# A perceiver layer on one core: the span attention's minimum, and the steps behind it, written into other stretches of the half batches

## The chip, the cores and the metric

The kernel runs on one core of a Trainium2 chip, in 32-bit floating point. A core has five engines with a queue each: TensorE (PE, with its weight loads shown apart as PEld), VectorE (DVE), ScalarE (ACT), GpSimd (POOL) and SyncE (SP), which here only issues DMAs. PSUM, into which TensorE writes, has eight banks; VectorE and ScalarE read them, GpSimd doesn't. The metric is the device time of one execution in microseconds (us), as the median of several runs.

## The reference

The input x has 32 batches of 64 rows of 256, the context 32 batches of 1601 rows of 256. One layer is computed, in three parts, each added to x:

```python
x = x + cross_attention(layernorm(x), ctx)   # 16 heads of 16, mask, softmax over 1601 keys
x = x + span_attention(layernorm(x))         # below
x = x + ffn(layernorm(x))                    # a shared gated layer and 8 experts, 2 for each row
```

Span attention gives each row and head a mean and a softness, and attends within the batch's 64 rows:

```python
span = h @ W_span.T                      # two numbers for each row and head
mean = sigmoid(span[..., 0]) * 64
soft = softplus(span[..., 1])
scores = -soft[..., None] * (pos - mean[..., None]) ** 2
attn = softmax(scores)                   # over 64 positions
out = (attn @ value) @ W_out.T           # value = h @ W_val.T, by heads
```

## The kernel before

**Half batches.** Cross attention is done for 8 heads at a time: a half batch n is (batch b, c = 0 or 1), 64 in all, in the loop at L763. Within one pass of the loop TensorE computes the scores of half batch n + 1, the keys and values of batch b + 1, and the values' products of half batch n - 1, while the softmax of n is under way:

- `scores` (L529): the 13 blocks of 124 keys in three groups of 4, 5 and 4, one PSUM bank for each of four head pairs (and, for the group of 5, one more bank and the spare half of another). VectorE adds the mask and takes them to the buffer `prob` (L570, and L563 for the fifth block), between them the running maxima over blocks (`maximum`, L587, into `mrun`, the last into `mx`); the first of the maxima is a copy on ScalarE (`first_maxima`, L579).
- `turned_maxima` (L594, pm) transposes `mx` on TensorE as soon as it is there, `maxima_of_rows` (L601) reduces on VectorE, `maxima_along_rows` (L609 on TensorE, copy mb L613 on ScalarE) spreads the result.
- `less_maxima` (L618) subtracts on GpSimd, four times; `exponentials` (L623) follows on ScalarE, four times, the last one in the next pass of the loop.
- `values` (L633) multiplies by the values, in two rounds of 104 small products; `project_keys` and `project_values` (L492) make keys and values of the next batch, and ScalarE copies them out (kT L507, v L524).

**The order is written out by hand** (`manual_schedule`, L729): each of PE, DVE, Activation and Pool executes its instructions in the order in which the program writes them. The pool of PSUM banks for all of this, `ps_x` (L392), has 6 banks; `mm_bank` takes one for each product, and it comes free when its reader has run.

**The stretches.** A pass of the loop has three stretches. In the first, `run(3n)` stands behind the first subtraction of maxima and before the second round of `values`; in the second, `steps(1)` stands behind the key and value projections and the second subtraction, before the exponential of pair 1; in the third, `steps(2)` stands at the end. `run` (L695) executes what is on the agenda for that stretch, in the order in which it was put there, and each generator says how many stretches later its next step is due.

**Tiles.** Two batches make a tile t of 128 rows (16 tiles). When the last half batch of a tile is done (`finish_steps`, L702), `span_steps` (L242) is put on the agenda. It has 23 steps, and the tables STEPS, LAST_BUT_TWO, LAST_BUT_ONE and LAST (L231 to L236) give the stretch of each, counted from the half batch 4t + 4; the last three are those of tiles 13, 14 and 15. The steps by their index in the tables:

| index | step | engine, line |
|---|---|---|
| 0 | output product po, addition to x, statistics | PE L248, DVE L251, L197 |
| 1 to 3 | spread, norm xn_h, transposition tr_h and copy to hT | POOL L205, ACT L214, PE L221, ACT L260 |
| 4, 5 | psp, span and z; exponential of z | PE L264, DVE L270, ACT L278 |
| 6 | sixteen small operations to mean and soft ("held") | DVE L291 to L303 |
| 7 | difference of positions and mean | POOL L308 |
| 8 | square; product with soft | ACT L312, POOL L313 |
| 9 | minimum `least` over 64 positions | DVE L316 |
| 10 to 13 | exponentials with their sums, 4 heads a step | ACT L320 |
| 14, 15 | reciprocal of the sums; product with it | DVE L325, POOL L327 |
| 16 | values pval, copies to vbd | PE L336, ACT L343 |
| 17 | transposition psa of the probabilities, copies to aT | PE L354, ACT L356 |
| 18, 19 | products po2 and po3, addition to x, statistics, x_kept | PE L364, L374, DVE L377, SP L379 |
| 20 to 22 | spread, norm xn_f, transposition tr_f and copies to xfT | POOL L205, ACT L214, PE L221, ACT L387 |

A tile's steps reach over 24 stretches and a new tile begins every 12, so two tiles are under way at a time: stretch 15 of one tile is stretch 3 of the next. The queries of a later tile (`query_steps`, L449) run at stretches 3 to 7 too (norm xn_q, transposition tr_q, copy xnT L458, product pq, four copies L471). `sc`, on which steps 7 to 17 work, has one buffer.

**The end.** In the last half batch (L826 on) there are no more projections; TensorE fills in the shared gated layer (`unit`, L675, reads xfT; `gate`, L678, on ScalarE and VectorE) between the last tiles' steps, at stretches given by the tables `begin` and `gated` (L847). Then follow the experts (L912, L930), 84 us of TensorE.

## Time and profile before

| | |
|---|---|
| median of 3 runs | 1527.41 us (1525.89 to 1528.43) |
| the profiled execution | 1530.65 us, of which the trace spans 1528.8 us |
| mean granted TensorE clock | 0.992 |
| busy share of the span | PE 96%, PEld 70%, DVE 80%, POOL 73%, ACT 62% |
| chain that ended last | PE 77%, DVE 18%, ACT 2%, issue 2% |
| half batches in the steady part | 20.4 to 22.0 us each |
| from the last pm (1360.31) to the experts (1442.39) | 82 us |

A row of a timeline gives the start (us from the first instruction), the time taken, engine, line, operation, output <- inputs with their shapes, and the number of like instructions; in brackets stands how long the engine had idled before, and what ended that. A row of the waits gives the idle time in all, how often, and the longest. A row for a stretch of time gives its length, then the busy time of PE, PEld, DVE, ACT and POOL with the number of instructions, the granted clock of TensorE (1.00 is full speed), the share of the DMA engines and GB/s.

### The profile page before, as it was taken

How to read it: one execution, taken by the hardware profiler on the slowest of the kernel's cores; microseconds unless marked ns; L12 is line 12 of the kernel's file. 1: busy time of each engine (PE TensorE's matmuls, PEld its weight loads, DVE VectorE, ACT ScalarE, POOL GpSimd, SP SyncE). 2: the span in 40 equal slices, each digit the busy share in tenths (PEclk: the TensorE clock that was granted, in tenths of full speed). 3: DMA queues.
4: the chain of work that ended last, by engine and by line, in shares of the span. 5: the costliest groups of instructions: out<-in, count | busy, mean ns of one | idle time of the engine just before them, and what ended most of it. 6: DMA issues, size and time to landing. Idle time of an engine off the chain costs nothing.

```text
span 1528.8 us, 62985 instructions
## 1 busy us (share of the span) xinstructions
PE 1469.1 (96%) x28600; PEld 1069.2 (70%) x28600; DVE 1224.9 (80%) x2332; ACT 947.6 (62%) x1725; POOL 1121.4 (73%) x508
## 2 busy tenths in 40 slices
PE   8999999999999999999999999999999999988999
PEld 5677767677776767776767767676777777654587
DVE  4889898989888898989898888988898888873100
ACT  3565667666767666666757676666766676756311
POOL 1777788888787878888887878777888778852700
PEclk9999999999999999999999999999999999999899
DMA  5111111111111101111111111011111111005100
GB/s 173 44 37 46 46 46 46 50 38 49 49 49 50 45 25 40 53 46 44 44 50 49 50 49 46 23 42 53 37 51 46 49 46 36 3 6 159 59 28 28
DMA packets 52076, 73.82 MB, mean 48 GB/s; under 512 B 3812, under 2 KB 51040, under 8 KB 51680
## 3 DMA queue, kind: packets, MB, share of 16 engines
q1 hardware_dynamic: 50992, 69.00, 14.8%
q8 instruction: 225, 3.69, 1.0%
q10 hardware_dynamic: 816, 0.79, 0.2%
q14 instruction: 43, 0.35, 0.1%
HBM read 65.57 MB, written 4.19 MB: 46 GB/s over the span
## 4 chain that ended last, share of the span: by engine, by line
PE 77%; DVE 18%; ACT 2%; issue 2%; DMA 0%; POOL 0%; ACTq 0%; POOLq 0%; DVEq 0%
PE pk L492 20%; PE pv L492 18%; PE psc L546 11%; PE pvs L633 10%; DVE mrun L587 8%; DVE prob L570 5%; PE py L930 4%; PE pm L594 2%; PE u L662 2%; PE pb L609 2%; PE ph L912 2%; DVE least L316 1%; PE pq L463 1%; PE psa L354 1%; PE po L248 1%
## 5 line engine op out<-in xcount | busy, mean ns | idle before, releaser
L618 POOL TENSOR_TENSOR prob<-prob,mb 124x1664 f32<-124x1664 f32 x252 | 939.5, 3753 | 222.3 <-ACT mb L613 189.0
L570 DVE TENSOR_TENSOR prob<-psc,madd 124x512 f32<-124x512 f32 x768 | 506.2, 680 | 67.9 <-PE psc L546 66.7
L587 DVE TENSOR_TENSOR mrun<-prob,mrun 124x512 f32<-124x512 f32 x704 | 486.5, 691 | 28.3 <-ACT mrun L579 15.5
L623 ACT ACTIVATE prob<-prob 124x1664 f32<-124x1664 f32 x256 | 406.8, 1590 | 143.2 <-POOL prob L618 140.6
L492 PE MATMUL pk<-ct,wkT_sb 128*32 128x372 f32 (+1 forms) x2512 | 388.6, 490 | 5.6 <-DMA wkT_sb<-in_wkT 5.5
L492 PE MATMUL pv<-wvT_sb,ct 128*124 128x256 f32 x3524 | 380.9, 379 | 0.1
L492 PEld LDWEIGHTS pv<-wvT_sb,ct 128*124 128x124 f32 x3524 | 273.0, 132 | 108.8 <-issue 11.6
L546 PE MATMUL psc<-qbd,kT 32*124 32x128 f32 x6400 | 243.6, 280 | 10.7 <-issue 8.4
L492 PEld LDWEIGHTS pk<-ct,wkT_sb 128*32 128x32 f32 (+1 forms) x2512 | 149.2, 127 | 137.0 <-issue 92.7
L546 PEld LDWEIGHTS psc<-qbd,kT 32*124 32x124 f32 x6400 | 203.1, 181 | 49.1 <-issue 27.4
L524 ACT COPY v<-pv 124x512 f32<-124x512 f32 (+1 forms) x224 | 124.6, 557 | 181.9 <-PE pv L492 181.9
L633 PE MATMUL pvs<-prob,v 124*17 124x64 f32 x13312 | 212.7, 220 | 2.7 <-issue 2.7
L633 PEld LDWEIGHTS pvs<-prob,v 124*17 124x17 f32 x13312 | 195.4, 98 | 24.4 <-issue 16.5
L507 ACT ACTIVATE kT<-pk,cols 128x372 f32<-128x372 f32 (+2 forms) x256 | 148.0, 589 | 87.9 <-PE pk L492 87.7
L320 ACT ACTIVATE sc<-sc,least 128x64 f32<-128x64 f32 x256 | 85.8, 342 | 3.2 <-DVE least L316 3.2
L932 DVE SCALAR_TENSOR_TENSOR ot<-py,prob 128x256 f32<-128x256 f32 x16 | 6.8, 424 | 75.7 <-PE py L930 66.1
L594 PE MATMUL pm<-cst,mx 124*128 124x124 f32 x256 | 42.2, 285 | 22.7 <-DVE mx L587 18.9
L662 PE MATMUL u<-xfT,sw_sb 128*128 128x512 f32 x128 | 59.7, 615 | 0.9 <-ACT xfT L387 0.9
L579 ACT COPY mrun<-prob 124x512 f32<-124x512 f32 x64 | 38.4, 599 | 29.4 <-DVE soft L303 26.4
L546 PE MATMUL pvs<-qbd,kT 32*124 32x128 f32 x256 | 55.1, 294 | 0.0
L609 PEld LDWEIGHTS pb<-cst,mc 128*124 128x124 f32 x256 | 29.0, 135 | 37.3 <-DVE mc L601 29.0
L563 DVE TENSOR_TENSOR prob<-psc,madd_fifth 124x256 f32<-124x256 f32 x64 | 27.0, 422 | 32.2 <-PE pvs L546 29.1
(125 smaller groups left out, 1246.7 us busy)
## 6 DMA issues: line engine op xcount, KB each, us to landing
ct<-in_ctxT SPq DMA_DIRECT2D x64, 372.0 KB, 3.2
ct<-in_ctxT SPq DMA_DIRECT2D x32, 496.0 KB, 5.1
ct<-in_ctxT SPq DMA_DIRECT2D x32, 361.0 KB, 3.9
w<-in_w SPq DMA_DIRECT2D x16, 256.0 KB, 7.7
x<-in_x SPq DMA_DIRECT2D x16, 128.0 KB, 2.3
x_kept<-x SPq DMA_DIRECT2D x16, 128.0 KB, 2.3
prob<-x_kept SPq DMA_DIRECT2D x8, 256.0 KB, 5.3
out<-ot SPq DMA_DIRECT2D x16, 128.0 KB, 1.9
```

The lines of the kernel that those rows point to most:

```text
L320: nc.scalar.activation(sc[:, h, :], sc[:, h, :], AF.Exp, bias=least[:, h : h + 1], scale=-1.0, accum_out=total[:, h : h + 1],)
L492: nc.tensor.matmul(out[at:end], lhsT=lhsT[:, at:end], rhs=rhs, start=start, stop=stop, **(dict(tile_position=(0, at)) if tiled else {}),)
L507: nc.scalar.activation(kTs[c][:, k0 : k0 + kn], ps[:, :kn], AF.Identity, bias=cols[:, B_K + c : B_K + c + 1])
L524: nc.scalar.copy(vs[b % 2][:kn, 2 * u : 2 * u + n, :, :DK], ps[:kn, : n * D].rearrange("p (n h d) -> p n h d", n=n, d=DK),)
L546: product = nc.tensor.matmul(ps[:CHUNK, at * P : (at + 1) * P], lhsT=kTs[c][32 * j : 32 * j + 32, k0 : k0 + CHUNK], rhs=qbd[b // 2][32 * j ...
L570: nc.vector.tensor_tensor(pair_of(n, j)[:, c0 : c0 + 4, :].rearrange("p k (e q) -> p k e q", e=2), pss[j][:CHUNK].rearrange("p (k e q) -> ...
L587: nc.vector.tensor_tensor(dst, block_of(n, k), run, ALU.max)
L594: nc.tensor.transpose(ps[:, j * CHUNK : (j + 1) * CHUNK], m[:CHUNK, j, :], ident[:CHUNK, :CHUNK])
L618: engine.tensor_tensor(sj, sj, m[:CHUNK, j, None, :].to_broadcast([CHUNK, NKC, P]), ALU.subtract)
L623: nc.scalar.activation(pair_of(n, j), pair_of(n, j), AF.Exp)
L633: nc.tensor.matmul(pvs[32 * j : 32 * j + DK + 1, c, :, r, :], lhsT=v[:kn, k, 8 * c + h, :], rhs=pair_of(n, h // 2)[:kn, k, (h % 2) * S : ( ...
L662: nc.tensor.matmul(ps, lhsT=w[:, c, hc * P : (hc + 1) * P], rhs=xfT[:, c, :, slot], start=(c == 0), stop=(c == 1),)
```

## The change

The new tables, and two steps of `span_steps` in another place:

```diff
-    STEPS = (3, 4, 5, 6, 7, 8, 9, 10, 11, 12, 13, 14, 15, 16, 18, 19, 20, 21, 23, 24, 25, 26, 27)
+    STEPS = (3, 4, 5, 6, 7, 8, 9, 11, 12, 15, 16, 17, 18, 19, 20, 20, 21, 22, 23, 24, 25, 26, 27)
     LAST_BUT_TWO = (
-        3, 4, 5, 6, 7, 8, 9, 10, 11, 12, 12, 13, 14, 15, 16, 17, 17, 18, 20, 21, 22, 23, 24,
+        3, 4, 5, 6, 7, 8, 9, 11, 12, 13, 13, 14, 15, 16, 17, 17, 17, 18, 20, 21, 22, 25, 27,
     )
-    LAST_BUT_ONE = (2, 2, 3, 4, 5, 5, 6, 7, 8, 9, 10, 10, 10, 10, 11, 11, 12, 13, 14, 15, 15, 16, 17)
-    LAST = (2, 2, 3, 4, 5, 6, 8, 9, 10, 11, 12, 12, 12, 12, 13, 13, 14, 15, 16, 17, 17, 18, 19)
+    LAST_BUT_ONE = (
+        2, 2, 3, 4, 5, 5, 6, 7, 8, 9, 10, 11, 12, 13, 14, 14, 14, 15, 16, 17, 17, 18, 19,
+    )
+    LAST = (2, 2, 3, 4, 5, 6, 8, 9, 10, 11, 12, 12, 12, 12, 13, 13, 13, 15, 16, 17, 17, 18, 19)
...
             yield next(waits)
-        nc.vector.reciprocal(total, total)
-        yield next(waits)
-        nc.gpsimd.tensor_tensor(sc, sc, total[:, :, None].to_broadcast(full), ALU.mult)
-        yield next(waits)
 
 
         pval = mm_bank(f"pval_{t}")
...
+        yield next(waits)
+        nc.vector.reciprocal(total, total)
+        yield next(waits)
+        nc.gpsimd.tensor_tensor(sc, sc, total[:, :, None].to_broadcast(full), ALU.mult)
         yield next(waits)
```

The values' product (index 16 before) now comes ahead of the reciprocal and the product with it, so that index 14 is pval, 15 the reciprocal and 16 the product. For tiles 0 to 12 (STEPS) the stretches are:

| step | before | after |
|---|---|---|
| difference; square and product with soft | 10; 11 | 11; 12 |
| minimum | 12 | 15 |
| exponentials | 13, 14, 15, 16 | 16, 17, 18, 19 |
| reciprocal; product | 18; 19 | 20; 21 |
| pval | 20 | 20 |
| psa | 21 | 22 |

All others stay. Tile 13 has its minimum and exponentials a stretch later (13; 13 to 16), and its last norm and transposition at 25 and 27 instead of 23 and 24. Tile 14 has its exponentials at 10, 11, 12 and 13 instead of all at 10, and what follows two to three stretches later. Tile 15 has pval at 13, with the reciprocal, instead of at 14. No instruction is added or taken away, except that ScalarE loads a table where it has to change between functions.

## The prediction

> **What bounds the kernel now.** I read five views in this order: the waits of TensorE, the chain that ended last around 700 to 800 us, the timeline of VectorE and ScalarE there, the groups, and the stretches with their granted clock. The work repeats every four half batches (84.14 us in the four stretches 701.59 to 785.73). I call them first to fourth half (n mod 4 = 0 to 3) and write +x for microseconds since that half's first transposition of maxima (pm, L594): 701.59, 722.29, 742.64, 763.70.

> ```profile
> PE pm L594 <- DVE mx L587: 18.9, 15, 2.4
> PE psc L546 <- issue: 8.4, 12, 1.6
> 701.59:722.29 20.70, 19.34 (x417) 13.89 (x413) 19.70 (x36) 14.13 (x32) 17.83 (x8) 1.00 0.08 24
> 722.29:742.64 20.35, 20.35 (x430) 14.75 (x430) 17.91 (x32) 14.79 (x35) 16.23 (x10) 1.00 0.24 69
> 742.64:763.70 21.06, 21.06 (x461) 16.09 (x457) 18.15 (x34) 14.61 (x24) 18.16 (x7) 1.00 0.06 21
> ```

> The first two rows are waits of TensorE (sum, times, longest). The others are three halves: length, then busy time of TensorE, its weight loads, VectorE, ScalarE, GpSimd. TensorE is busy without a break in the second and third half: anything that holds it there is lost outright. Only in the first half is VectorE the bound (19.70 busy of 20.70), and TensorE loses 1.36 there, waiting for the last maximum:

> ```profile
> 705.24 0.42 DVE L377 TENSOR_TENSOR x<-x,po 128x256 f32<-128x256 f32 x1 [0.43 <-PE po L374]
> 706.26 1.19 DVE L316 TENSOR_REDUCE least<-sc 128x16 f32<-128x1024 f32 x1
> 708.68 0.42 DVE L563 TENSOR_TENSOR prob<-psc,madd_fifth 124x256 f32<-124x256 f32 x1
> 722.29 0.64 PE L594 MATMUL pm<-cst,mx 124*128 124x124 f32 x4 [1.36 <-DVE mx L587]
> ```

> **Part 1: the minimum leaves the first half (stretch 12 to 15).** It takes 1.19 on VectorE there, but that isn't the gain. Without it the two maxima that follow end 1.33 after +4.70, at +6.03; the next operation (L563) reads scores that TensorE begins at +5.12, and in the second and third half, where VectorE waits for them, L563 starts 1.42 after they begin (5.34 to 6.76; 4.70 to 6.12). So it starts at +6.54 instead of +7.09. From L563 to the end of the last maximum VectorE now needs 13.56 (708.68 to 722.24). Gain: **0.55**, not 1.19; the half becomes 20.15. Tiles 1 to 12 have this (tile 0's minimum lies in such a wait already): 12 x 0.55 = **-6.6**. Bounds: 0, and 12 x 1.36 = -16.3 if the whole wait goes.

> In the second half the minimum comes ahead of po's addition (L251): its steps were put on the agenda first. VectorE idles there 0.73 for po, so 0.46 of 1.19 shows, L563 goes from +6.76 to about +7.05, and the last maximum ends near +19.6, before TensorE asks at +20.35. Cost 0; if that cover were gone, 13 x 1.19.

> **Part 2: what follows moves with it, and this decides.** The sixteen exponentials (four parts, L320) go from stretches 13 to 16 (two parts in the first half, two in the second) to 16 to 19: two in the second, two in the third. A part is 4 x 0.335 = 1.34 on ScalarE (four starts, 720.93 to 722.25). ScalarE works in the order written. Its rows at the turn from second to third half, and TensorE's second round of scores:

> ```profile
> L320 ACT ACTIVATE sc<-sc,least 128x64 f32<-128x64 f32 x256 | 85.8, 342 | 3.2 <-DVE least L316 3.2
> 740.51 1.59 ACT L623 ACTIVATE prob<-prob 124x1664 f32<-124x1664 f32 x1
> 742.50 0.59 ACT L214 ACTIVATE xn_q<-x,neg_q,rstd_q 128x256 f32<-128x256 f32 x1
> 743.42 1.59 ACT L623 ACTIVATE prob<-prob 124x1664 f32<-124x1664 f32 x1 [0.33 <-POOL prob L618]
> 746.03 0.60 ACT L579 COPY mrun<-prob 124x512 f32<-124x512 f32 x1
> 746.55 0.38 ACT L260 COPY hT<-tr_h 128x256 f32<-128x256 f32 x1
> 747.56 1.03 PE L546 MATMUL psc<-qbd,kT 32*124 32x128 f32 x29
> ```

> Stretch 17 puts a part after the exponential of 740.51 and before the two norms (xn_h, xn_q); stretch 18 puts another before hT's copy, since the older tile's steps run first. The sum, from the second half's pm: exponential at +18.22, part at +19.72, norms at +21.06 and +21.55, last exponential at +22.04 instead of +21.13. That is the third half's +1.69 instead of +0.78. Then 1.57 to kT's copy, 0.57 to mb's, 0.47 to mrun's, 0.52 (746.03 to 746.55) to the new part, 1.34 for it, 0.38 for hT's copy: +6.54 instead of +4.29.

> Who waits: the pool has six PSUM banks. The scores of L546 take five and the key projection behind them the sixth, and two of the six are tr_h's and tr_q's, which only the copies L260 and L458 free. So one of them must be free for the scores' second round at +4.92. Now it is so by 0.6; after the change TensorE stands until +6.57, a new wait of **1.65** in a half with no slack, of which about 0.2 comes earlier, where the values' products (due +3.12) wait for the exponential that ends at +3.28. Tiles 0 to 12: 13 x 1.65 = **+21.5**. Lower bound, if the last exponential weren't late: 1.65 - 0.91 = 0.74, or +9.6. Below that I see nothing: the part stands ahead of the copy in the program.

> **Part 3: GpSimd, and steps that cost nothing.** The product with soft (L313, 1.90) goes behind the first subtraction of maxima in the first half; the last subtraction then ends at +21.66, where GpSimd now idles 4.50. This makes the second half's mb about 0.75 late; nothing there needs it before +5.55. The normalising product (L327) leaves the third half for the fourth, the difference (L308) goes behind the last subtraction there: both in idle time (3.63 in the fourth half). The probabilities' transposition (psa) moves one stretch on in the fourth half, 0.87 of TensorE in either place; its ScalarE copies are due before the key projection at +12.4 and end at +12.2. If that cover fails, it costs tenths. The square (1.07) goes behind mrun's copy, before a wait of 3.35. The reciprocal (0.24) moves into VectorE's 1.22 wait. SP's queue keeps its order, and no DMA moves except tile 14's x_kept, 4 us later, read only at the end. Sum 0, bounds -2 and +4.

> **Part 4: the end.** Tile 13's minimum stays in its half (n = 60) but goes behind L563: 1.19 - 0.55 = **+0.6**. In the last half tile 14's exponentials fill 5.4 us of ScalarE while TensorE stands:

> ```profile
> 1381.76 0.69 PE L221 MATMUL tr_f<-cst,xn_f 128*128 128x128 f32 x2 [6.89 <-ACT xn_f L214]
> 1416.66 1.97 PE L354 MATMUL psa<-cst,sc 128*128 128x128 f32 x8 [2.67 <-POOL sc L327]
> ```

> Split in four, the po product of tile 15 and two units start at about 1376.4. But two more table loads appear (1.28 each), tile 14's po3 now comes behind three units (8.8 us) and ends near 1397 against 1392.4, and VectorE's 3.1 us of small steps for tile 15 stand behind it, as early as now (1398.1). What remains is some 2 us on ScalarE ahead of tile 15's square. I take **-1.5**, bounds -5 and +3.

> **Part 5: instruction gaps and the clock.** Some third halves already lose 0.2 to 0.9 at this place for no release that the profile shows ("issue"); a wait swallows them: **-1.5**. The other way:

> ```profile
> 1040.23 0.64 PE L546 MATMUL psc<-qbd,kT 32*124 32x128 f32 x9 [1.61 <-issue]
> 1037.05:1040.46 3.41, 1.80 (x83) 1.50 (x72) 1.15 (x2) 3.41 (x4) 2.83 (x2) 1.00 0.68 236
> 1040.46:1043.88 3.42, 3.42 (x16) 2.01 (x12) 2.95 (x5) 0.03 (x1) 0.53 (x1) 0.50 0.02 5
> ```

> A single gap of 1.61 amid values' and scores' products was followed by 3.41 us at a granted clock of 0.50, about 1.6 lost; a gap of 1.68 at 534.46 was not, and none of the 1.36 waits was. About half of the thirteen new waits lie whole in one such stretch ((3.41 - 1.65) / 3.41); with half of those answered, 3 x 1.6 = **+4.8**; bounds 0 and 7 x 1.6 = 11.2. [...]

> **Sum.** -6.6 + 21.5 + 0 + 0.6 - 1.5 - 1.5 + 4.8 = +17.3 on an execution of 1530.65 (span 1528.8), 0.2% above the median of 1527.41, where the same gives **1544.7**.

> **Rivals.**
> - *Half the wait.* The last exponential isn't late, so only the part counts: 13 x 0.74 = 9.6, and no clock answer: 9.6 - 6.6 + 0.6 - 1.5 - 1.5 = +0.6, with a few clock answers 1528 to 1535; I put it at 1531. For it: VectorE or GpSimd may shift ScalarE's order of readiness. Against: ScalarE's rows are back to back there.
> - *Faster.* VectorE's relief is all: hT's copy is done by +4.92. Then 0 for Part 2: -6.6 + 0.6 - 1.5 = -7.5, 1520. It decides if a bank other than tr_h's and tr_q's is free; six banks and six takers speak against it.
> - *The clock answers nearly every wait:* 7 x 1.6 instead of 3 x 1.6: 1551, and to 1558 if windows lie badly.
> - *No effect of the main move:* the first half stays 20.70, since something else holds VectorE: +6.6, 1551.

> **Chances.** Forecast (1536 to 1549) 0.57; clock or no relief 0.18; half the wait 0.14, about a third of it within 0.2% (1524.4 to 1530.5, what a measurement here can tell from no change); faster 0.09; unforeseen, slower 0.02. So faster 0.09, within 0.2% 0.05, slower 0.86. Range 1530 to 1556: it leaves out the faster case and the tails.

> **What would show it.** TensorE's wait for mx in the first half at 0.8 instead of 1.36; a new wait "PE psc <- ACT hT" or "ACT sc" of 1.65, thirteen times, at +4.9 of the third half; third halves of 22.7; more stretches at clock 0.50; the last exponential at +1.7. Wrong, if TensorE runs on at +4.9 in the third half.

## The result, and the profile after

The changed kernel takes **1529.97 us** (median of 20 runs, 1527.28 to 1535.66) against 1527.45 for the kernel before (20 runs, 1523.71 to 1530.32): a ratio of **1.0022, 95% interval 1.0012 to 1.0032**. It is slower, but by 2 to 5 us instead of the 17 of the forecast, and its median lies just under the range's low end of 1530. The profiled execution took 1529.89 us (span 1528.1, clock 0.996). That of before, 1530.65, was 3 us above its median; so the pair of profiles differs by -0.7 where the medians differ by +2.5.

All lines behind the tables, but for the moved steps, are two higher in the changed kernel (L546 is L548 now). Its waits of TensorE (sum, times, longest):

```profile
PE pm L596 <- DVE mx L589: 14.1, 16, 2.4
PE psc L548 <- ACT hT L262: 9.7, 11, 0.9
PE psc L548 <- issue: 5.6, 8, 1.6
```

The first was 18.9, the third 8.4; the second is new: it is the wait of Part 2. First to fourth half of the same tile as in the prediction (length, then busy PE, PEld, DVE, ACT, POOL, the granted clock, DMA share, GB/s):

```profile
704.97:725.12 20.15, 19.34 (x416) 13.92 (x413) 18.68 (x35) 12.47 (x15) 17.89 (x9) 1.00 0.06 20
725.12:745.48 20.36, 20.36 (x431) 14.77 (x431) 18.84 (x33) 13.33 (x28) 17.09 (x11) 1.00 0.24 70
745.48:768.05 22.57, 21.70 (x461) 16.48 (x457) 18.17 (x34) 18.21 (x47) 16.82 (x6) 1.00 0.06 20
768.05:788.64 20.59, 20.59 (x469) 15.22 (x465) 18.89 (x42) 12.58 (x18) 17.01 (x6) 1.00 0.25 71
```

The fourth half before:

```profile
763.70:785.73 22.03, 20.96 (x469) 15.37 (x465) 18.99 (x42) 13.29 (x18) 16.70 (x5) 1.00 0.24 70
```

Against 20.70, 20.35, 21.06 and 22.03: the first half is shorter by 0.55, the third longer by 1.51, and the fourth, of which the prediction expected nothing, shorter by 1.44. The turn into the third half, ScalarE and then TensorE's second round of scores:

```profile
746.65 0.59 ACT L214 ACTIVATE xn_q<-x,neg_q,rstd_q 128x256 f32<-128x256 f32 x1
747.14 1.58 ACT L625 ACTIVATE prob<-prob 124x1664 f32<-124x1664 f32 x1
748.62 0.66 ACT L509 ACTIVATE kT<-pk,cols 128x496 f32<-128x496 f32 x1
749.64 0.59 ACT L581 COPY mrun<-prob 124x512 f32<-124x512 f32 x1
750.16 0.35 ACT L322 ACTIVATE sc<-sc,least 128x64 f32<-128x64 f32 x1
...
751.50 0.36 ACT L262 COPY hT<-tr_h 128x256 f32<-128x256 f32 x1
751.91 1.03 PE L548 MATMUL psc<-qbd,kT 32*124 32x128 f32 x26 [0.87 <-ACT hT L262]
```

The last exponential starts at +1.66 (forecast +1.69), the third part stands ahead of hT's copy, which ends at +6.38 (+6.54), and TensorE goes on at +6.43 (+6.57). The chain is as predicted.

Where the time went, from the lengths of all half batches of both profiles, with the clean length of a half taken from those without a gap (first 20.70 and 20.15, third 21.05 and 22.57, fourth 20.59 in both), in us:

| | before | after | difference |
|---|---|---|---|
| 12 first halves, n = 12 to 56 | 251.84 | 243.83 | -8.0 (-6.6 clean; the rest is mostly the half-clock window at 1040.46, which isn't there after) |
| third halves, n = 10 and 14 to 58 | 279.59 | 294.73 | +15.1 (13 x 1.52 = +19.8 clean; surplus over clean 5.9 before, 1.3 after: -4.6) |
| 12 fourth halves, n = 15 to 59 | 257.90 | 252.20 | -5.7 (surplus over clean 10.8 before, 5.1 after) |
| n = 60 to 62, and from there to the experts | 149.55 | 147.48 | -2.1 |
| sum | | | -0.6 (the spans: -0.7) |

The "surplus" is what the halves take beyond their clean length. Part of it is idle time of TensorE that the profile puts down to "issue", which I call gaps (before, 3.1 of the third halves' 5.9 and 6.9 of the fourth halves' 10.8; 0.9 more in the fourth, at n = 43, is put down to the last maximum). The rest is busy time: products that take longer than in a clean half. So the open question was: why did half of the new wait's price come back in this surplus, in the third halves and above all in the fourth, where on TensorE nothing but psa's place had changed?

### The profile page after: what moved, and what is told of

The parts are those of the page before. It is cut to its first block, busy times and chain, and to the rows that moved or that the text cites. A ratio compares the mean times of both kernels' runs of the same rounds, so it can differ in the third digit from the quotient of the medians.

```text
span 1528.1 us, 62953 instructions
## 1 busy us (share of the span) xinstructions
PE 1470.4 (96%) x28600; PEld 1071.4 (70%) x28600; DVE 1222.8 (80%) x2332; ACT 947.7 (62%) x1727; POOL 1119.0 (73%) x508
## 4 chain that ended last, share of the span: by engine, by line
PE 72%; DVE 17%; ACT 8%; issue 2%; POOL 0%; DMA 0%; ACTq 0%; DVEq 0%; POOLq 0%
PE pv L494 18%; PE pk L494 18%; PE psc L548 11%; PE pvs L635 8%; DVE mrun L589 7%; DVE prob L572 6%; PE py L932 4%; ACT sc L322 3%; PE pm L596 2%; ACT prob L625 2%; PE u L664 2%; PE ph L914 2%; PE pb L611 2%; PE pq L465 1%; PE psa L356 1%
## 5 line engine op out<-in xcount | busy, mean ns | idle before, releaser
L548 PE MATMUL psc<-qbd,kT 32*124 32x128 f32 x6400 | 246.6, 280 | 17.0 <-ACT hT L262 9.7
L548 PEld LDWEIGHTS psc<-qbd,kT 32*124 32x124 f32 x6400 | 204.7, 182 | 54.7 <-issue 19.7
L548 PE MATMUL pvs<-qbd,kT 32*124 32x128 f32 x256 | 54.9, 294 | 0.0
L565 DVE TENSOR_TENSOR prob<-psc,madd_fifth 124x256 f32<-124x256 f32 x64 | 27.0, 421 | 32.2 <-PE pvs L548 31.1
```

The lines of the kernel that those rows point to most:

```text
L548: product = nc.tensor.matmul(ps[:CHUNK, at * P : (at + 1) * P], lhsT=kTs[c][32 * j : 32 * j + 32, k0 : k0 + CHUNK], rhs=qbd[b // 2][32 * j ...
```

## The experiments

Three theories stood against each other. **A**: the wait lets TensorE's instructions catch up, and this takes away the gaps of the third half and, through it, of the fourth. **B**: the fourth half's gaps went because psa left its first stretch. **C**: the gaps differ by chance between executions. Each ratio below is against runs of the kernel before on the same chip.

**late_third_part.** In `span_steps` and `run`, so that the third part comes behind the copies of hT and xnT:

```diff
-            yield next(waits)
+            wait = next(waits)
+            yield -wait if part == 1 and t < NTILE - 3 else wait
...
-        for steps in agenda.pop(stretch, []):
+        for steps in agenda.pop(stretch, []) + behind.pop(stretch, []):
...
-            if wait:
+            if wait and wait < 0:
+                behind[stretch - wait].append(steps)
+            elif wait:
                 agenda[stretch + wait].append(steps)
```

> This kernel is the changed one, with one step of tiles 0 to 12 elsewhere: the third part of the exponentials (stretch 18) is written behind the copies of hT and xnT in the third half, and so no longer stands ahead of hT's copy on ScalarE. What stays of the wait at the second round of scores (1.52 us in the changed kernel's profile) should be what the late exponential of pair 3 makes: about 0.3, all by the other part that moved; third halves of 21.3 instead of 22.57, if nothing else fills the gap. Theory A (the 1.52 wait swallows the instruction gaps of the third half, 5.9 us of surplus over the clean length before and 1.3 after, and through it those of the fourth half, 10.8 before and 5.1 after): the wait falls by 13 x 1.2 = 15.6, and the gaps come back by 4.6 + 5.7, so about 5.5 below the changed kernel: 1524.5. Theory B (the fourth half's gaps went because psa's transposition is a stretch later, which stays so here): third halves' 4.6 come back, the fourth half's don't: 11 below, about 1519. Theory C (the gaps differ by chance between executions): 15.6 below on the average, less what the gaps of one execution say: 1514 to 1519.

Measured: 1518.61, ratio 0.9919 (0.9897 to 0.9940). Third halves are 21.25 clean, with a surplus of 5.7 again; the fourth halves' sum stays at 253.2. So the part ahead of hT's copy is what the third half pays for, all but 0.2. The third halves' gaps do come back with the wait gone (A is right there), the fourth halves' don't (B).

**psa_back.** The changed kernel with

```diff
-    STEPS = (3, 4, 5, 6, 7, 8, 9, 11, 12, 15, 16, 17, 18, 19, 20, 20, 21, 22, 23, 24, 25, 26, 27)
+    STEPS = (3, 4, 5, 6, 7, 8, 9, 11, 12, 15, 16, 17, 18, 19, 20, 20, 20, 21, 23, 24, 25, 26, 27)
```

> The changed kernel, with the transposition psa of the probabilities back in stretch 21 for tiles 0 to 12 (the product with the reciprocal then in stretch 20). Theory A (the fourth half's gaps shrink because the wait in the third lets the instructions catch up): nothing changes, 1530, the fourth halves' surplus over 20.59 stays near 5 us in all. Theory B (they shrink because psa left the first stretch of the fourth half): the surplus goes back to about 10.8, the time to 1535.5. Theory C: 1530, with a surplus anywhere between 5 and 11.

Measured: 1533.98, ratio 1.0031 (1.0017 to 1.0045). The fourth halves' sum is 257.41, a surplus of 10.3: B, in the profile. The medians, each against its own runs of before, give only some 1.4 to 2.7 for it.

**psa_only.** The kernel before with psa's stretch alone changed, 21 to 22:

```diff
-    STEPS = (3, 4, 5, 6, 7, 8, 9, 10, 11, 12, 13, 14, 15, 16, 18, 19, 20, 21, 23, 24, 25, 26, 27)
+    STEPS = (3, 4, 5, 6, 7, 8, 9, 10, 11, 12, 13, 14, 15, 16, 18, 19, 20, 22, 23, 24, 25, 26, 27)
```

> The kernel before the change, with nothing but psa moved, from stretch 21 to 22 in tiles 0 to 12. Theory A: no difference beyond 1 us, 1527.5, fourth halves' surplus near 11. Theory B: the fourth halves lose 5 to 6 us of surplus, 1522. Theory C: 1527.5, with a surplus anywhere.

Measured: 1523.21 against 1528.80, ratio **0.9958** (0.9943 to 0.9973): 4 to 9 us. The fourth halves' sum is 252.03. The same place of the program in both, first before, where psa stands ahead of the values' products:

```profile
766.28 1.04 PE L354 MATMUL psa<-cst,sc 128*128 128x128 f32 x8
767.25 1.65 PE L633 MATMUL pvs<-prob,v 124*17 124x64 f32 x104
...
770.70 0.81 PE L546 MATMUL psc<-qbd,kT 32*124 32x128 f32 x19 [1.07 <-issue]
```

and then psa_only, where it doesn't:

```profile
765.44 1.65 PE L633 MATMUL pvs<-prob,v 124*17 124x64 f32 x104
...
767.24 1.03 PE L546 MATMUL psc<-qbd,kT 32*124 32x128 f32 x29
768.32 1.52 PE L492 MATMUL pk<-ct,wkT_sb 128*128 128x372 f32 x4
```

All 29 products run on here; before, TensorE stopped for 1.07 among them. B is shown: psa's move, which the prediction had put at nothing, is a gain of about 5.6 in the kernel before. Nor is it chance between executions (C): in the four kernels with psa in stretch 21 (before, psa_back and, below, least_and_exps_late and end_only) the fourth halves' surplus is 9.4 to 10.8, and in the seven with psa in 22 and nothing put ahead of the half batches (after, late_third_part, psa_only and, below, second_part_early, two_parts_ahead, late_and_psa and trh_later) it is 5.0 to 6.1.

**least_and_exps_late.** late_third_part with the difference, the product with soft and psa where they were before the change, the second part of the exponentials in stretch 16 too, and the normalising product in 20:

```diff
-    STEPS = (3, 4, 5, 6, 7, 8, 9, 11, 12, 15, 16, 17, 18, 19, 20, 20, 21, 22, 23, 24, 25, 26, 27)
+    STEPS = (3, 4, 5, 6, 7, 8, 9, 10, 11, 15, 16, 16, 18, 19, 20, 20, 20, 21, 23, 24, 25, 26, 27)
```

> Only what pays, by the theory that the change is two things with opposite signs: tiles 0 to 12 have the minimum in stretch 15, two parts of the exponentials in 16, the third in 18 behind the copies of hT and xnT, the fourth in 19; difference, square, product with soft, psa and all that follows are in the stretches of the kernel before; the end is the changed one. By the profile pair: first halves -6.6, the end -2.1 in all, no wait for hT's copy, so 1527.5 - 8.7 = 1519, less up to 2 if gaps fall too. If an exponential part in stretch 16 (two instead of one, ahead of everything of stretch 17) makes the exponential of pair 3 late after all, a wait of 0.3 to 0.9 in each third half stays, +4 to +12: 1523 to 1531. Theory B for the gaps (psa is back in stretch 21 here) gives 1519 and a fourth-half surplus near 11, theory A the same time with a third-half surplus near 6.

Measured: 1520.56, ratio 0.9926 (0.9905 to 0.9948). First halves 20.16, third halves 21.05 clean with a surplus of 6.4, fourth halves 256.5. The minimum's move is a gain of its own.

**second_part_early.** The changed kernel with the exponentials' four parts in other stretches:

```diff
-    STEPS = (3, 4, 5, 6, 7, 8, 9, 11, 12, 15, 16, 17, 18, 19, 20, 20, 21, 22, 23, 24, 25, 26, 27)
+    STEPS = (3, 4, 5, 6, 7, 8, 9, 11, 12, 15, 16, 16, 18, 19, 20, 20, 21, 22, 23, 24, 25, 26, 27)
```

> The changed kernel, with the second part of the exponentials of tiles 0 to 12 in stretch 16 instead of 17, so that it no longer stands ahead of the two norms and the last exponential on ScalarE; the third part still stands ahead of hT's copy. This asks how the wait of 1.52 is made up. By the prediction's lower bound (1.65 - 0.91) the third half keeps a wait of 0.74 and is 21.8 long instead of 22.57: 13 x 0.77 = 10 less, about 1520 if a shorter wait swallows the gaps as well, 1522 to 1524 if part of them comes back. Rival: the last exponential is late because GpSimd's subtraction is late, and not because of the part; then nothing changes: 22.57 and 1530.

Measured: 1526.49, ratio 0.9980 (0.9968 to 0.9992); third halves 22.30, not 21.8. The last exponential still starts at +1.37, with no part ahead of it. Its row in this kernel:

```profile
742.45 0.59 ACT L214 ACTIVATE xn_q<-x,neg_q,rstd_q 128x256 f32<-128x256 f32 x1
743.96 1.59 ACT L625 ACTIVATE prob<-prob 124x1664 f32<-124x1664 f32 x1 [0.93 <-POOL prob L620]
```

and GpSimd's two subtractions ahead of it, before the change and in this kernel:

```profile
735.89 7.49 POOL L618 TENSOR_TENSOR prob<-prob,mb 124x1664 f32<-124x1664 f32 x2
```

```profile
736.44 7.49 POOL L620 TENSOR_TENSOR prob<-prob,mb 124x1664 f32<-124x1664 f32 x2
```

They start 6.75 ahead of the third half's pm before, and 6.15 ahead of it here (pm at 742.64 and 742.59). So GpSimd is 0.60 late by the steps that moved to it, and the part on ScalarE hid that: of the 0.88 by which the exponential is late in the changed kernel, 0.60 has two causes side by side. With GpSimd's steps left as they were, least_and_exps_late has it at +0.77 again.

**two_parts_ahead.** The wait made longer:

```diff
-    STEPS = (3, 4, 5, 6, 7, 8, 9, 11, 12, 15, 16, 17, 18, 19, 20, 20, 21, 22, 23, 24, 25, 26, 27)
+    STEPS = (3, 4, 5, 6, 7, 8, 9, 11, 12, 15, 16, 17, 18, 18, 20, 20, 21, 22, 23, 24, 25, 26, 27)
```

> The changed kernel, with the fourth part of the exponentials of tiles 0 to 12 in stretch 18 too, so that two parts (2 x 1.34) stand ahead of hT's copy in the third half: the wait of 1.52 becomes 2.86, of which 2.2 in one piece (0.88 now). By the waits alone: third halves of 23.9, and 13 x 1.34 = 17.4 more than the changed kernel, 1547, or 1 less if the last of the third halves' gaps goes too. Prediction's clock term: a standstill longer than the 1.61 that was answered at 1040.46 lies whole in a stretch of 3.41 us in (3.41 - 2.2) / 3.41 = 35% of cases, 4 to 5 of 13, and half to all of these are answered by 3.41 us at a clock of 0.50 (1.6 lost each): 3.5 to 7.5 more, 1551 to 1555, with half-clock windows between 230 and 1270 in the profile. Rival: no standstill of this kind is answered (no half-clock window there but the one near 1040): 1547.

Measured: 1558.98, ratio 1.0191 (1.0170 to 1.0212). Third halves are 23.90 where nothing else happens, with 2.2 idle in one piece. Four of the thirteen waits were answered by the clock, one of them twice (n = 10, 22, 26, 38: 25.55, 25.55, 25.85 and 26.97 long). The stretch with the wait of n = 10 and the one after it:

```profile
243.20:246.61 3.41, 1.21 (x30) 1.01 (x34) 1.23 (x2) 3.30 (x19) 3.41 (x2) 1.00 0.02 5
246.61:250.02 3.41, 3.41 (x24) 2.16 (x19) 2.43 (x5) 1.32 (x1) 3.41 (x2) 0.50 0.00 0
```

TensorE is busy 1.21 of 3.41, and runs the next 3.41 at half the clock. These answers cost 8.3 in the third halves of the profile, against the 3.5 to 7.5 that were expected, and the time lies above the 1551 to 1555; one more stretch at half the clock, in n = 48, and a slower kernel before in this set of runs (1529.13 instead of 1527.45) make up most of the rest. So the prediction's clock term is real at 2.2 in one piece; none of the changed kernel's waits, with 0.88 in one piece, was answered (its granted clock is 1.00 from 9.94 to 1361.61).

**end_only.** The kernel before for tiles 0 to 12, the changed tables and order of steps for tiles 13 to 15 (`shares` holds the reciprocal and the product with it).

```diff
+        if t < NTILE - 3:
+            yield from shares()
         pval = mm_bank(f"pval_{t}")
...
+        if t >= NTILE - 3:
+            yield from shares()
```

> The kernel before the change in tiles 0 to 12, stretch by stretch, with the changed end: tiles 13, 14 and 15 by the changed tables and in the changed order of steps. By the five profiles so far (from n = 60 to the experts 149.6 and 148.8 with the old end; 147.5, 148.4, 145.2 with 1.4 given back later, and 147.5 with the new one) the new end gives 1.0 to 2.0: 1525.5 to 1526.5. The prediction's sum of +0.6 and -1.5 would give 1526.6. Rival: the spread of these profiles is chance and the end gives nothing: 1527.5.

Measured: 1528.36 against 1529.13, ratio 0.9992 (0.9978 to 1.0005). The end's part lies between a gain of 3.4 and a loss of 0.8; the prediction's -0.9 fits, and so would nothing.

**late_and_psa.** least_and_exps_late with psa in stretch 22.

```diff
-    STEPS = (3, 4, 5, 6, 7, 8, 9, 10, 11, 15, 16, 16, 18, 19, 20, 20, 20, 21, 23, 24, 25, 26, 27)
+    STEPS = (3, 4, 5, 6, 7, 8, 9, 10, 11, 15, 16, 16, 18, 19, 20, 20, 20, 22, 23, 24, 25, 26, 27)
```

> The kernel least_and_exps_late with psa in stretch 22 instead of 21: the minimum in stretch 15, two parts of the exponentials in 16, the third in 18 behind hT's and xnT's copies, the fourth in 19, psa in 22, the changed end, all else as before the change. If the effects add, psa's move takes the fourth halves' gaps away (5.5 us, as in psa_only) from 1520.6: 1515. Rival: the supply of instructions that is short in these halves is short elsewhere then, and the gaps move into other halves: 1518 to 1520.

Measured: **1515.37** against 1529.13, ratio 0.9910 (0.9892 to 0.9927), better than both kernels; the effects add. Its first, third and fourth half, in the same columns as above:

```profile
698.12:718.28 20.16, 19.35 (x417) 13.92 (x413) 18.69 (x35) 12.23 (x16) 18.15 (x9) 1.00 0.07 22
...
738.63:759.68 21.05, 21.05 (x460) 16.08 (x456) 18.16 (x34) 17.11 (x40) 17.12 (x7) 1.00 0.06 22
759.68:780.28 20.60, 20.60 (x469) 15.22 (x465) 18.90 (x42) 13.06 (x18) 17.56 (x6) 1.00 0.25 74
```

It has the short first half without the long third one, and TensorE runs through the third and fourth.

What the gaps are was still open. Two kernels were to tell whether they grow with the number of short products in a row.

**psa_twice.** The kernel before, with

```diff
-            for i in range(4):
+            for i in (0, 1, 2, 3) * (2 if t < NTILE - 3 else 1):
```

> The kernel before the change, with the eight transpositions psa of tiles 0 to 12 done twice over, the second time to the same place, so that 16 short products instead of 8 stand ahead of the values' products in the fourth half, at the place where the gaps are. The eight more cost 0.97 each time by the row of psa (1.04 for 8, of which the last is drawn out): 13 x 0.97 = 12.6 in any case. Theory (TensorE's instructions don't come fast enough where a run of short products gets longer with no standstill before it): the gaps behind grow too, from 5 of 12 fourth halves with 0.4 to 1.1 to nearly all 12 with 1 or more, 6 to 10 more: fourth halves' sum 276 to 280, the time 1546 to 1550. Rival (the gaps belong to places in the program or to chance): the sum 269 to 270, the time 1540.

Measured: 1533.74 against 1527.55, ratio 1.0035 (1.0023 to 1.0047). The fourth halves' sum is 265.41: 0.87 more clean in each (21.46), and a surplus of 7.9, less than before. The time is 6.2 more, below the rival's 1540 too: of the 12.6 that were expected in any case, 10.4 stand in the 12 fourth halves, and 2.9 less surplus there takes part of it back. The theory of more short products falls; and the gaps are at other places now: n = 23, 27 and 31 near +22, none near the end of n = 43 and 47.

**trh_later.** late_and_psa, with tr_h in stretch 7 and psp in 8:

```diff
-    STEPS = (3, 4, 5, 6, 7, 8, 9, 10, 11, 15, 16, 16, 18, 19, 20, 20, 20, 22, 23, 24, 25, 26, 27)
+    STEPS = (3, 4, 5, 7, 8, 8, 9, 10, 11, 15, 16, 16, 18, 19, 20, 20, 20, 22, 23, 24, 25, 26, 27)
```

> The kernel late_and_psa, with the transposition tr_h (two products) and hT's copy of tiles 0 to 12 in stretch 7 instead of 6, and psp in 8 instead of 7, so that of the four short transpositions ahead of the values' products in the third half only tr_q's two are left there. Theory (as for psa: fewer short products in a row, no gaps): the third halves' surplus over the clean length, 6.5 in all, falls to 1 to 4, and the time from 1515.4 to 1510 to 1513. Rival (the gaps belong to the place): 6.5 and 1515. Against both: psp and the statistics behind it come a stretch later, next to the operations of mean and soft in the first stretch of the fourth half; if these hold up VectorE there, up to 0.5 for each fourth half, 6 more.

Measured: 1518.34, ratio 0.9938 (0.9924 to 0.9952), so slower than late_and_psa, by 3 us in the medians and 4 by the two ratios. The third halves' surplus falls only from 6.5 to 5.7, and the clean length of the twelve up to n = 54 rises from 21.05 to 21.31, for a reason that wasn't traced. A miss for the theory once more.

So I counted in the trace: each record of a product or a weight load on TensorE in order, and where the gaps without a releaser (those for which the profile names nothing that ended them, only "issue") stand in that count. In the kernel before, from n = 2 on, they stand at 2225, 5283, 9865, 12411, 13939, 15975, 17503, 21065 and so on: differences of 3058, 4582, 2546, 1528, 2036, 1528, 3562, which are close to 12, 18, 10, 6, 8, 6 and 14 times 254.5. So they would stand where one piece of TensorE's instructions ends and the next begins; I call such a place a joint, and the row of joints a ladder. The last two kernels move the work against that count, and add only a microsecond or two ahead of it.

**shift_32.** late_and_psa with, ahead of all half batches,

```diff
+    for _ in range(32):
+        nc.tensor.matmul(pb[:32, D : D + 32], lhsT=ident[:, :32], rhs=ident[:, :32], start=True, stop=True)
```

> The kernel late_and_psa, with 32 products of 32 x 32 that nothing reads put ahead of all half batches (behind the product pbv, near 28 us), about 1 us of TensorE, once. In the eleven profiles so far every gap of TensorE over 0.15 us without a releaser, from n = 2 to 61, stands at a multiple of about 254.5 records (products and weight loads) from the one at n = 2. Theory: these are the joints of pieces in which TensorE's instructions come. Then the extra 64 records leave the joints at the same counts and put other work there: no gap any more at n = 14 (+5.9), n = 24 (+1.7) and n = 47 (+22.3), where every kernel had them, and instead some of n = 19 (+6.3), 22 (+4.9 to 5), 26 (+5.4), 42 (+4.7), 43 (+5.2), 50 (+5.1), 54 (+5.7); all again on the ladder of 254.5. The time may go either way by up to 5 from 1516. Rival: the gaps belong to the work (to a place in a half batch) or to a time on the chip: the same halves as before have them, and the time is 1516.

**shift_64.** The same with 64.

> As shift_32, with 64 products, 128 records, about half a piece, and about 2 us of TensorE. Theory: the gaps at n = 14, 24 and 47 (+22.3) are gone, and the joints fall on short products at n = 10 (+6.4), 23 (+5.1), 30 (+5.0), 34 (+5.6), 47 (+4.9), 51 (+6.3), 54 (+4.9), 58 (+5.4), of which some show a gap; the time 1517, up to 5 either way. Rival: the same halves as before, 1517.

Measured: 1517.33, ratio 0.9911 (0.9894 to 0.9927), and 1520.92, ratio 0.9942 (0.9924 to 0.9960). The expectations had the sizes wrong by two: such a product leaves two records of a product and two of a load (pbv's two products ahead of them stand as x4 in the timeline), so the shifts are 128 and **256** records, half a piece and a whole one. With that the theory is borne out twice. Half a piece: the gaps at n = 14, 24 and 47 are gone, and new ones stand at n = 19, 26, 30, 31, 35, 40, 51, 54, 58 and 59 (30, 51, 54 and 58 are four of the eight that were worked out for a shift of 128 records; 10, 23, 34 and 47 show none). A whole piece: the gaps are back in the old halves (n = 2, 6, 14, 18, 19, 22, 24, 30, 42, 43, 46, 47, 61; only n = 26's is missing, and one at n = 11, as in the changed kernel, is added), each 256 records further in the count. The gap at the end of n = 47, in late_and_psa,

```profile
1028.91 0.93 PE L549 MATMUL psc<-qbd,kT 32*124 32x128 f32 x23
1031.73 0.50 PE L549 MATMUL psc<-qbd,kT 32*124 32x128 f32 x9 [1.90 <-issue]
```

at the end of n = 47 in shift_32, where the 32 products run in one piece,

```profile
1027.41 1.15 PE L549 MATMUL psc<-qbd,kT 32*124 32x128 f32 x32
```

and in shift_64, split between the same two products as in late_and_psa:

```profile
1032.85 0.93 PE L549 MATMUL psc<-qbd,kT 32*124 32x128 f32 x23
1035.96 0.50 PE L549 MATMUL psc<-qbd,kT 32*124 32x128 f32 x9 [2.18 <-issue]
```

## Why the prediction was wrong

The direction and the chain were right, the size was not. **The steps that failed are "Sum 0" of Part 3, in which psa's move stood at nothing, and Part 5, the gaps and the clock.** Their three terms make 13.6 of the 14.8 by which the forecast of +17.3 missed the +2.5 of the medians, and the wait's term 1.7. Beside the terms, what the profiles and runs showed:

| term | predicted | shown |
|---|---|---|
| Part 1, first halves | -6.6 | -6.6: 20.70 to 20.15; L565 starts at +6.54, as predicted |
| Part 2, the wait | +21.5 | +19.8: 13 x 1.52 |
| Part 3, psa | 0 | -5.7 in the profiles, -5.6 alone (psa_only); psa_back's medians give only -1.4 to -2.7 |
| Part 4, the end | -0.9 | -2.1 in the profiles; end_only: -3.4 to +0.8 |
| Part 5, gaps of the third half | -1.5 | -4.6 (1.3 left of 5.9) |
| Part 5, the clock | +4.8 | 0 |

With -5.7 for psa and the predicted -0.9 for the end, the right column makes +2.0 (with -2.1 for the end, +0.8); the medians differ by 2.5.

- **Part 1** holds to the hundredth. TensorE's wait for the last maximum is 0.81 in the changed trace, as foreseen, and the second half hides the minimum at no cost. least_and_exps_late shows that the gain is there by itself.
- **Part 2**: the chain is right row by row. The wait came 0.13 shorter, since the exponential, the copies and the part follow each other a little closer than the sum of their rows. The *lower bound* was wrong: without the part ahead of it the exponential would still have been 0.60 late, because of GpSimd. In Part 3 the prediction saw GpSimd's mb about 0.75 late, and found nothing in the second half that needs it; the third half's exponential does. This cost nothing in the changed kernel only because ScalarE was later still.
- **Part 3**: "0.87 of TensorE in either place" is true, and isn't the cost. The profile of before had 1.07 of idle time behind psa and the values' products that follow it, in the half whose length (22.03 in this tile) the prediction passed over, while it did look for gaps in the third half.
- **Part 5, gaps**: the mechanism, that a wait swallows them, was right, and the term too small by three. In every kernel with a wait of 1.25 or more in the third half (after, psa_back, second_part_early, two_parts_ahead) the surplus there is 1.0 to 1.7 (the clock's answers taken off), in every other one 5.7 to 6.8. The prediction's 1.5 is half of the 3.1 that stand as idle time in the third halves of its own profile, and their lengths show 5.9.
- **Part 5, the clock**: the term was taken from one row and held against the wrong length. Of the 1.65 only 0.88 is idle in one piece; the rest is values' products that wait one by one (1.82 for the 104 instead of 1.65) and the drawn-out end of the four products ahead of the gap (0.47). Held against the row's 1.61 it had to be compared as the profile shows it, as 0.88. two_parts_ahead shows that the term exists: with 2.2 in one piece it is 8.3 us.
- **The rivals.** "Half the wait" gave nearly the right time, 1531, for a wrong reason: the wait came whole. "Faster" and "no effect" fall by the rows above, "the clock answers nearly every wait" too.

What stays open: what holds up TensorE's next instructions where psa stands ahead of the values' products. At the joint of n = 27 the instruction packet that lands ahead of it (the last section tells of these) starts 3.9 us after the joint before it was passed in before and psa_back, and 1.3 after it in after, psa_only and late_and_psa; psa itself takes one of these 2.7 us. Open are also why twice as many transpositions cost no more than that, and the 0.26 in trh_later's third half.

## What to carry to other kernels

Read the idle time that no release explains half by half, before and around every place that a change touches: here a step that "only moves" was worth more than the end of the kernel. The new wait cost less than its length here, where it stands over such gaps (+19.8 for the thirteen, with 4.6 less surplus in the same halves), and the longer one cost more: in two_parts_ahead, with 2.2 idle in one piece, four of thirteen were followed by 3.41 us at half the clock. So compare a wait as the idle time that falls into such a stretch (0.88 in the changed kernel), not as the delay of what comes next (1.65 in the forecast, 1.52 measured). And a change that is two moves of opposite sign should be taken apart: the minimum's move and psa's gave 14 us together with the end (1515.4) once the one part of exponentials stood behind the copy that TensorE waits for.

## What the runs showed of the hardware

**Joints in TensorE's instructions.** In the fourteen profiles there are 202 gaps of TensorE over 0.15 us without a releaser between n = 2 and n = 61, and in each profile all of them stand within 6 records of one ladder of 254.5 to 254.7 recorded products and loads. With the semaphore and drain instructions of TensorE's queue counted in (345 in the kernel before), the step is 256: all 202 stand within one record of the same count modulo 256 (the 21 of the kernel before and the 13 of the changed one at 193 or 194). The page of the kernel before has packets that fit (queue, number, MB, share of the DMA engines):

```profile
q8 instruction: 225, 3.69, 1.0%
```

Each is of 16,384 bytes; 225 times 256 is 57,600, and TensorE's queue has 57,545 instructions in this trace, no other one more than 2,600. In the traces each of the 202 gaps ends 0.96 to 1.62 us (median 1.42) after the last such packet has landed, and no joint is passed less than 0.9 us after its packet landed. The gap of 1.07 in n = 35 of the kernel before ends at 770.70; its packet starts at 768.18 and lands at 769.15. So I take the gaps for waits for TensorE's next instructions. A shift of the work by 256 records brings them back to the same work, a shift by 128 doesn't. Most joints show no gap: of some 207 in this part of each profile 10 to 21 do, of 0.15 to 2.2 us, mostly among values' and scores' short products (104 of the values' take 1.65). What gaps are left are not free: late_and_psa still shows 7.1 us of "issue" ahead of scores' products.
